# Issuing the load of the w2 sums for batch 14's last step behind the first eight adjacency rows of the final joined product

## The chip, the cores and the metric

The kernel runs on one core of a Trainium2 chip. The metric is the device time in microseconds of one execution; lower is better. The engines are named as in the profile: PE (matrix products; PEld is its weight load), DVE (vector), ACT (scalar, activations), POOL and SP. SP computes nothing here: it issues the DMAs, in the order in which the program names them.

## What is computed

For x of shape (16, 1024, 256), 16 batches of 1024 nodes with 256 channels, two layers run, each with a residual and a layer norm over the channels. The first is an attention whose queries come from a product with an adjacency matrix weighted by the likeness of the nodes. The second, in which the change lies, is a pair of graph convolutions:

```python
h = relu(x @ w1_loop + adj @ (x @ w1_neigh) + b1)      # 256 -> 128 channels
h = relu(h @ w2_loop + adj @ (h @ w2_neigh) + b2)      # 128 -> 256 channels
x = layernorm(x + (x + h) * 0.5)                       # adj is 1024 x 1024, the same for all batches
```

All is in float32.

## The kernel before

The batches pass through a pipeline written out by hand. While the attention of batch b runs, the first graph convolution of batch b-1 and the second of batch b-2 are computed together. Their common factor is the adjacency matrix, so the class `Joined` puts both into one block product by Strassen's scheme (in Winograd's form): the 2 x 2 blocks of the adjacency and four sums of these blocks are multiplied in seven products instead of eight. The eight factors of the adjacency lie in DRAM as `far_adj`, named "00", "01", "10", "11" (the blocks, transposed) and 1, 2, 3, 4 (their sums). Each is two tiles ("rows") of 128 x 1024 floats, 512 KB each. `fetch` (line 193) loads both tiles of a factor, one DMA each, issued by SP (line 198).

The last product of the second convolution, with w2, is done by the same scheme (`seventh_part`, line 967, and `last_products`, line 978). It needs four sums of blocks of w2 and one row of the bias, 320 KB in all, which were computed once at the start and lie in DRAM as `w2_sums`. `load_sums` (line 948) takes a row tile and loads them (line 950).

`Joined.run` (line 1137) goes in this order. Products 1, 2, 6, 7, 5, 4 and 3 (line 1134) read the factors "00", "10", 2, 3, 1, 4 and "11". Between them, functions of other stages are called from a table that the caller passes (`turn_to`). After product 2 the bias of the first half of the channels is put into the PSUM bank `third`, and `load_sums` is called for the older batch (`c2`). After product 4, `block_sums` (line 953) makes the left sums, and `bias(second, c2.b2_step)`, an ACT copy of line 1142, reads the fifth block of the loaded sums. Then come half of product 3, three steps of `last_products` (line 971 on PE, copies on ACT at lines 984, 989 and 992, additions on DVE at lines 986, 993 and 975), the other half of product 3, and the rest.

The final step, lines 1447 to 1461, has no attention beside it: `c1` is batch 15, `c2` batch 14, and `c3` and `c4` are batches 13 and 12, whose results still have to be normalized and stored. SP's order in this step is: fourteen adjacency tiles (line 1449), two more of block "01" (line 1450), the residual x of batch 14 (`c2.load_x`, line 850), the store of batch 12's result (`c4.finish`, line 1018), the residual x of batch 15 (`c1.load_x`, line 850), the sums of w2 (line 950), the store of batch 13's result (line 1018). The x tiles come from a pool of three buffers, so that batch 15's x takes the one from which batch 12's result is stored.

Row tiles, which hold adjacency tiles, sums, snapshots of PSUM and the like, come from a pool of 31 buffers of one size (`row_tile`, line 99), handed out in turn: the first instruction that writes a tile waits until the buffer's former content is no longer read. After the seven products, `ending` (line 1029) computes the second convolution of batch 15 and its layer norm, and stores it piece by piece.

Of the kernel before, what the change touches and what calls it, by code (L numbers as in the profile page):

```python
# [18 lines left out]
def kernel(  # L19
# [68 lines left out]
    def half_psum(name):  # L88
        return big_psum(name)[:, 0:FB]
# [4 lines left out]
    def load_x(b, name):  # L94
        xb = xpool.tile([P, NT, C], F32, tag="x", name=f"x_{name}")
        nc.sync.dma_start(out=xb, in_=x[b].rearrange("(t p) c -> p t c", p=P))
        return xb

    def row_tile(name):
        return work.tile([P, N], F32, tag="row", name=name, bufs=ROWS)  # L100
# [107 lines left out]
    def fetch_quarters(name, ready=None):  # L208
        return {ij: (ready or {}).get(n) or fetch(n, name) for ij, n in QUARTERS.items()}
# [67 lines left out]
    class NodeSums:  # L277


        def __init__(self, q, xb, name):  # L280
            self.q, self.name = q, name
            self.square = squares[len(taken) % 2]
            taken.append(name)
            q.c_col = self.square[:, 0:NT]
            for t in range(NT):
                nc.scalar.activation(xb[:, t, :], xb[:, t, :], AF.Identity, accum_out=self.square[:, t:t + 1])
# [118 lines left out]
    class KeysValues:  # L405
# [45 lines left out]
        def run(self, between=lambda: None, later=lambda: None):  # L451
            self.start()
            self.middle(between, later)
            return self.end()
# [387 lines left out]
    class GraphConv:  # L842


        def __init__(self, b, xT, nodes=None, x=None):
            self.b, self.xT, self.nodes, self.x = b, xT, nodes, x

        def load_x(self):
            self.x = xpool.tile([P, NT, C], F32, tag="x", name=f"x1_{self.b}")
# [253 lines left out]
    class Joined:  # L1103
# [33 lines left out]
        def run(self, between=None, last=None):  # L1137
            c1, c2, b = self.c1, self.c2, self.b
            between = between or {}

            def bias(bank, row):
                nc.scalar.copy(bank.rearrange("p (t c) -> p t c", c=P), row.unsqueeze(1).to_broadcast([P, TJ, P]))

            def turn_to(n):
                for f in between.get(n, ()):
                    f()

            first, third, second = (half_psum(f"hu_ps_{b}_{i}") for i in range(3))
            s12, s34 = (row_tile(f"snap_{b}_{k}") for k in range(2))
            p1, u1, u3, p7 = s12[:, 0:FB], s12[:, FB:N], s34[:, 0:FB], s34[:, FB:N]  # L1150
            c1.loop(third, 0, start=True)
            self.product(1, first, start=True)
            nc.scalar.copy(p1, first)
            turn_to(1)
            self.product(2, third)
            nc.vector.tensor_add(p1, p1, third)
            turn_to(2)
            if last:
                bias(third, b2_sb[:, ts(0, P)])
                c2.load_sums()  # L1160
            self.product(6, first, again=True)
            nc.scalar.copy(u1, first)
            c1.relu(0, p1)
            turn_to(6)
            self.product(7, second, start=True)
            nc.scalar.copy(p7, second)
            turn_to(7)
            self.product(5, first, again=True)
            nc.scalar.copy(u3, first)
            turn_to(5)  # L1170
            self.product(4, second, again=True)
            c2.uT = row_tile(f"uT_{c2.b}")
            add_upper = lambda: nc.vector.tensor_add(c2.uT[:, 0:FB], u1, second)
            add_lower = lambda: (last or nc.gpsimd).tensor_add(c2.uT[:, FB:N], u3, p7)
            if not last:
                add_upper()
                add_lower()
                turn_to(4)
                c1.loop(first, 1, again=True)
                self.product(3, first, again=True)  # L1180
                c1.relu(1, first)
                turn_to(3)
                return
            c2.block_sums(last, add_upper, add_lower)
            bias(second, c2.b2_step)
            turn_to(4)
            c1.loop(first, 1, again=True)
            self.product(3, first, again=True, steps=range(0, TJ // 2))
            rest = c2.last_products(third, second)
            self.product(3, first, again=True, steps=range(TJ // 2, TJ))  # L1190
            c1.relu(1, first)
            rest()
            turn_to(3)
            return third, second

    def run():
# [58 lines left out]
        for b in range(B):  # L1255
            more = b + 1 < B
            att = Attention(b, xB, qT, kT, v)
            c1, c2, c3 = (convs.get(b - k) for k in (1, 2, 3))
            both = Joined(c1, c2) if c2 else None
# [186 lines left out]
            convs[b] = GraphConv(b, norm.x1T, norm.nodes)  # L1446
        c1, c2, c3, c4 = (convs[B - k] for k in (1, 2, 3, 4))
        both = Joined(c1, c2)
        both.fetch("00", "10", 2, 3, 1, 4, "11")
        quarters = fetch_quarters("e", both.far)  # L1450
        c2.load_x()
        c1.inner()
# [10 lines left out]
    with tc.manual_schedule():  # L1463
        run()
# [67 lines left out]
```

## Time and profile before

| what | value |
|---|---|
| median of the runs | 2136.1 us |
| lowest and highest of 3 runs | 2135.74 and 2136.44 us |
| time of the profiled execution | 2135.35 us |
| span of the profiled execution | 2133.6 us |
| mean granted PE clock in it | 0.997 |
| PE busy | 2116.3 us (99%) |
| DVE busy | 1907.5 us (89%) |
| ACT busy | 1140.1 us (53%) |
| POOL busy | 359.0 us (17%) |
| DMA queue of the loads and stores | 61.2% of 16 engines |

The span runs from the first to the last instruction that the profile has; what lies around it is 1.75 us here. An engine's busy share is a mean over the whole program. All moments below are us from the start of the span. The final step, in which the change lies, covers roughly the last 78 us: its first adjacency load is issued at 2054.66 us.

### The profile page before, as it was taken

Reading aid. Unit: us, or ns where it says so; the run is one execution under the profiler, and the core shown is the slowest. Engines: PE = TensorE matmul, PEld = TensorE weight load, DVE = VectorE, ACT = ScalarE, POOL = GpSimd, SP = SyncE. Lnnn points to the kernel's source line nnn. Section 1 sums busy time; section 2 is a strip of 40 time slices with the busy share of each in tenths; the row PEclk is TensorE's granted clock in tenths of the full one; section 3 lists DMA queues with packets and bytes.
Section 4 is the critical chain, followed back from the end, with each engine's and each line's share of the span. In section 5 each row is a group of like instructions: output and inputs, shape, how many; then the busy total and the mean of one; then the engine's idle time right before and its main releaser. Section 6 shows DMA issues by size and latency. Waiting matters only on the chain.

```text
span 2133.6 us, 25172 instructions
## 1 busy us (share of the span) xinstructions
PE 2116.3 (99%) x8734; PEld 1037.2 (49%) x8734; DVE 1907.5 (89%) x2381; ACT 1140.1 (53%) x1669; POOL 359.0 (17%) x209
## 2 busy tenths in 40 slices
PE   9999999999999999999999999999999999999997
PEld 5344444545545455444454444544454444545454
DVE  7899999989999898998989989899898999989874
ACT  5745545556365563655635555454655546556322
POOL 2010120221303113031130301313012130221111
PEclk9999999999999999999999999999999999999998
DMA  9495666637549284592946829377293763925453
GB/s 222 120 170 193 135 221 146 186 107 141 203 125 272 74 165 169 137 262 70 201 141 150 241 69 233 109 163 228 75 259 103 153 212 106 268 87 107 165 192 112
DMA packets 613718, 346.39 MB, mean 162 GB/s; under 512 B 491984, under 2 KB 556880, under 8 KB 613584
## 3 DMA queue, kind: packets, MB, share of 16 engines
q1 hardware_dynamic: 613312, 344.45, 61.2%
q8 instruction: 71, 1.16, 0.2%
q14 instruction: 63, 0.52, 0.1%
q10 hardware_dynamic: 272, 0.26, 0.0%
HBM read 294.45 MB, written 50.20 MB: 162 GB/s over the span
## 4 chain that ended last, share of the span: by engine, by line
PE 98%; DMA 1%; DVE 1%; ACT 0%; POOL 0%; issue 0%; POOLq 0%; SPq 0%; ACTq 0%; DVEq 0%
PE s L702 21%; PE av L744 21%; PE g_ps L647 16%; PE hu_ps L1134 16%; PE v_ps L448 5%; PE k_ps L444 5%; PE hu_ps L971 4%; PE t_ps L857 3%; PE g_ps L574 3%; PE hu_ps L864 2%; PE h_ps L879 1%; PE u_ps L908 1%; DMA out_dram<-x 1%; PE h_ps L971 1%; DMA w_sums<-w_sums 0%; PE den_ps L764 0%
## 5 line engine op out<-in xcount | busy, mean ns | idle before, releaser
L723 DVE TENSOR_TENSOR acc<-acc,pr 128x1024 f32<-128x1024 f32 x384 | 472.2, 1230 | 37.4 <-DVE acc L723 1.4
L702 PE MATMUL s<-qT,kT 64*128 64x512 f32 x2048 | 449.7, 593 | 0.0
L744 PE MATMUL av<-pr,v 128*64 128x512 f32 x2048 | 447.0, 594 | 0.0
L709 ACT ACTIVATE pr<-s 128x1024 f32<-128x1024 f32 x392 | 390.7, 1115 | 75.6 <-PE s L702 75.6
L702 PEld LDWEIGHTS s<-qT,kT 64*128 64x128 f32 x2048 | 196.3, 187 | 232.7 <-issue 183.3
L744 PEld LDWEIGHTS av<-pr,v 128*64 128x64 f32 x2048 | 144.0, 137 | 297.4 <-issue 272.6
L361 POOL TENSOR_TENSOR rstd<-rstd,neg_half 128x32 f32<-128x32 f32 x16 | 99.3, 6203 | 1113.2 <-DVE rstd L359 1113.2
L1134 PE MATMUL hu_ps<-adj,R 128*128 128x512 f32 x480 | 214.3, 594 | 0.0
L560 ACT ACTIVATE wg<-c_row,c_sums 128x1024 f32<-128x1024 f32 x120 | 137.0, 1142 | 81.4 <-DVE den_part L731 60.3
L566 DVE SCALAR_TENSOR_TENSOR wg<-wg,adj 128x1024 f32<-128x1024 f32 x128 | 150.0, 1211 | 3.6 <-ACT wg L561 3.6
L707 ACT ACTIVATE pr<-s 128x512 f32<-128x512 f32 x240 | 142.4, 702 | 0.3 <-PE s L702 0.3
L1134 PEld LDWEIGHTS hu_ps<-adj,R 128*128 128x128 f32 x480 | 89.0, 190 | 100.9 <-issue 99.5
L561 ACT ACTIVATE wg<-wg 128x1024 f32<-128x1024 f32 x128 | 135.3, 1057 | 4.1
L860 ACT COPY t<-t_ps 128x1024 f32<-128x1024 f32 x16 | 16.2, 1012 | 189.6 <-PE t_ps L857 189.6
L647 PE MATMUL g_ps<-wg,S 128*128 128x512 f32 x224 | 115.5, 597 | 0.0
L647 PE MATMUL g_ps<-T,S 128*128 128x512 f32 x224 | 115.5, 597 | 0.0
L647 PE MATMUL g_ps<-wg,x 128*128 128x512 f32 x224 | 109.0, 599 | 0.0
L1134 PE MATMUL hu_ps<-adj,t 128*128 128x512 f32 x240 | 105.7, 592 | 0.0
L1125 POOL TENSOR_TENSOR R<-h 128x512 f32<-128x512 f32 x14 | 28.2, 2012 | 359.5 <-PE av L744 238.8
L721 DVE TENSOR_TENSOR acc<-pr,pr 128x1024 f32<-128x1024 f32 x64 | 77.5, 1211 | 12.3 <-ACT pr L709 12.3
L728 DVE STREAM_TRANSPOSE accB<-acc 128x1024 f32<-128x1024 f32 x64 | 79.7, 1245 | 2.2
L731 DVE TENSOR_REDUCE den_part<-accB 128x32 f32<-128x1024 f32 x64 | 78.1, 1220 | 2.2
(235 smaller groups left out, 3120.1 us busy)
## 6 DMA issues: line engine op xcount, KB each, us to landing
adj<-adjT SPq DMA_DIRECT2D x210, 512.0 KB
adj<-in_adj_dram SPq DMA_DIRECT2D x128, 512.0 KB
para<-in_L_gnn_para_dram SPq DMA_DIRECT2D x32, 512.0 KB
xB_a<-in_x_dram SPq DMA_DIRECT2D x128, 128.0 KB
x1d<-xB_a SPq DMA_DIRECT2D x128, 128.0 KB
x<-x1d SPq DMA_DIRECT2D x16, 1024.0 KB
xB<-in_x_dram SPq DMA_DIRECT2D x120, 128.0 KB
x<-in_x_dram SPq DMA_DIRECT2D x15, 1024.0 KB
```

Of the source, the lines that this page charges most:

```text
L444: nc.tensor.matmul(dst, self.a[0][n], self.w[n], start=not again, stop=True, skip_group_check=again)
L448: nc.tensor.matmul(dst[:, ts(t, P)], self.w[n][:, ts(t, P)], self.a[1][n], start=not again and t == 0, stop=True, skip_group_check=again o ...
L560: nc.scalar.activation(wg, self.c_row, AF.Abs, bias=self.c_col[:, t:t + 1], scale=-1.0)
L561: nc.scalar.activation(wg, wg, AF.Tanh, scale=-0.5 / C)
L566: nc.vector.scalar_tensor_tensor(wg, wg, 1.0, self.adj.pop(t), op0=ALU.add, op1=ALU.mult)
L647: nc.tensor.matmul(self.p[n], x_n[:, k, :], w_n, start=(k == 0), stop=(k == TJ - 1))
L702: nc.tensor.matmul(halves[s], self.kT[rows, pair, ts(mt, P)], self.qT[rows, pair, ts(j, FB)], start=True, stop=True)
L707: nc.scalar.activation(pr[:, ts(s, FB)], halves[s], AF.Exp)
L709: nc.scalar.activation(pr, ps, AF.Exp)
L723: nc.vector.tensor_add(self.acc, self.acc, prs[mt])
L744: nc.tensor.matmul(pav[s * HD:(s + 1) * HD, :], self.v[:, mt, pair * P + s * HD:pair * P + (s + 1) * HD], prs[mt][:, ts(s, FB)], start=(mt ...
L1134: nc.tensor.matmul(dst, self.x[n][:, k, :], of_rows(rows, k), start=(start and k == 0), stop=(k == TJ - 1), skip_group_check=again)
```

## The change

In the final step, `load_sums` for batch 14 is called when eight of the fourteen adjacency tiles ("00", "10", 2 and 3) have been issued, ahead of the six of 1, 4 and "11". `Joined.run` calls it only where it has not been called for this batch. In the steps before the final one nothing changes: there the sums are still loaded in `run`.

```diff
@@ class GraphConv
         def __init__(self, b, xT, nodes=None, x=None):
             self.b, self.xT, self.nodes, self.x = b, xT, nodes, x
+            self.w2 = None
 
         def load_x(self):
@@ class Joined, run
             turn_to(2)
             if last:
                 bias(third, b2_sb[:, ts(0, P)])
-                c2.load_sums()
+                if c2.w2 is None:
+                    c2.load_sums()
             self.product(6, first, again=True)
@@ the final step
         c1, c2, c3, c4 = (convs[B - k] for k in (1, 2, 3, 4))
         both = Joined(c1, c2)
-        both.fetch("00", "10", 2, 3, 1, 4, "11")
+        both.fetch("00", "10", 2, 3)
+        c2.load_sums()
+        both.fetch(1, 4, "11")
         quarters = fetch_quarters("e", both.far)
         c2.load_x()
```

The row tile of the sums is now the ninth that the final step takes, where it was the twenty-second; the tiles in between come one place later in the turn of the pool's buffers.

## The prediction

> **What bounds the kernel now.** I read the page first: PE is busy for 2116.3 us of a span of 2133.6 us, and the chain of work that ended last is PE for 98% of the span. So the change can only gain where PE stands still, and only the last step is touched. I therefore read the PE timeline from 2040 us to the end, for the last step and for the step before it, which runs the same code for batch 13.
>
> The PE timeline (start, us, engine, line, operation, count, and in brackets idle time and what ended it), first the earlier step, then the last one:
>
> ```profile
> 2047.44 1.05 PE L971 MATMUL hu_ps<-w2n_sb,uT 128*128 128x128 f32 x8
> 2048.33 1.06 PE L971 MATMUL h_ps<-w2l_sb,h1T 128*128 128x128 f32 x8
> 2049.23 2.98 PE L971 MATMUL hu_ps<-w_sums,last 128*128 128x128 f32 x24
> 2052.04 1.88 PE L1134 MATMUL hu_ps<-adj,R 128*128 128x512 f32 x4
> ...
> 2086.36 1.05 PE L971 MATMUL hu_ps<-w2n_sb,uT 128*128 128x128 f32 x8
> 2087.25 1.06 PE L971 MATMUL h_ps<-w2l_sb,h1T 128*128 128x128 f32 x8
> 2095.13 4.62 PE L971 MATMUL hu_ps<-w_sums,last 128*128 128x128 f32 x24 [6.83 <-ACT h L984]
> 2099.59 1.88 PE L1134 MATMUL hu_ps<-adj,R 128*128 128x512 f32 x4
> ```
>
> The same four groups stand in both; only in the last step is there a hole, 6.83 us ahead of the 24 products, and these then take 4.62 instead of 2.98 us. From 2040 to 2124 us PE has no other idle time of this size. The hole is put down to the ACT copy of line 984, so I read ACT's timeline:
>
> ```profile
> 2079.25 0.59 ACT L1169 COPY snap<-hu_ps 128x512 f32<-128x512 f32 x1 [2.85 <-PE hu_ps L1134]
> 2093.49 0.59 ACT L1142 COPY hu_ps<-w_sums 128x512 f32<-128x512 f32 x1 [13.65 <-DMA w_sums<-w_sums]
> 2094.01 0.58 ACT L904 COPY h<-h1n_ps 128x512 f32<-128x512 f32 x1
> 2094.49 0.59 ACT L984 COPY h<-hu_ps 128x512 f32<-128x512 f32 x1
> ```
>
> Line 984 was not late by itself: it stood in ACT's queue behind line 1142, the preload of a PSUM bank with the bias step, which waited 13.65 us for the sums of w2. Why these came so late is in the chain of waits in order of time (start, us, what):
>
> ```profile
> 2072.27 13.35 DMA out_dram<-x
> 2085.62 0.02 issue
> 2085.64 0.36 SPq L850
> 2086.00 0.05 issue
> 2086.05 0.02 SPq L950
> 2086.06 0.03 issue
> 2086.09 7.32 DMA w_sums<-w_sums
> ```
>
> SP's queue is in order. Line 850 loads the residual x of batch 15 into a buffer that batch 12's output store still reads until 2085.62; the load of the sums (line 950) needs nothing of that store, yet is issued behind it, and then takes 7.32 us beside a 1 MB load and a 1 MB store.
>
> **What the Trainium skill says.** "TensorE: Matmul & The Clock Gate", Part 1 (the HAM clock gate): after about 3.4 us idle the array falls to half clock, and needs about 3.4 us of work to come back. The windows of 1 us agree (busy us of PE, PEld, DVE, ACT, POOL, then the granted clock, DMA share, GB/s): idle from 2088.3, half clock from about 2091.8 (a mean of 0.92 in that window), full again at about 2098.7 (a mean of 0.66), 3.6 us after work resumed.
>
> ```profile
> 2090.00:2091.00 1.00, 0.00 (x0) 0.00 (x0) 0.00 (x0) 0.00 (x0) 0.00 (x0) 1.00 0.89 252
> 2092.00:2093.00 1.00, 0.00 (x0) 0.00 (x0) 0.00 (x0) 0.00 (x0) 0.00 (x0) 0.50 1.07 386
> 2097.00:2098.00 1.00, 1.00 (x6) 1.00 (x6) 0.00 (x0) 0.59 (x1) 0.00 (x0) 0.50 0.00 0
> 2099.00:2100.00 1.00, 1.00 (x8) 0.78 (x8) 0.00 (x0) 0.21 (x1) 0.00 (x0) 1.00 0.00 0
> ```
>
> "DMA: Bandwidth & Descriptors", Anatomy of one DMA: a semaphore wait happens on the issuing sequencer before dispatch, so a waiting issue holds all behind it. The 13.35 us above agree. The same page, Issuing engines are not separate DMA queues: all DMAs share 16 engines. Agreed too: the adjacency loads alone run at 401 to 422 GB/s from 2061 to 2077 us with the DMA share at 1.0.
>
> **The change part by part.**
>
> 1. *The late load goes.* Line 950 is skipped in this step's run, so line 1142 needs only what it needs in the earlier step: PSUM bank `second` free, that is, DVE's line 1173 (2083.61, 0.69 us). It runs at about 2084.35 to 2084.95, line 904 to 2085.5, and ACT is free. In the earlier step line 984 starts 1.14 us after the first group of 8 products starts (2048.58 against 2047.44) and the 24 products start 1.79 us after it. So here: copy at 2087.50, products at 2088.15 instead of 2095.13, which is 6.98 us. No hole above 3 us is left, so the clock stays full, and the 24 products reach line 1134 in 2.81 us (2052.04 - 2049.23) instead of 4.46 (2099.59 - 2095.13), which is 1.65 us. From there to the transposes of line 903 it takes 3.50 us in the last step and 3.51 in the earlier one. Sum 8.63 us. As a check over the whole piece: 2103.09 - 2086.36 = 16.73 against 2055.55 - 2047.44 = 8.11, a difference of 8.62.
>
> 2. *The early load comes.* One more issue on SP, 0.32 us (median of 15; 0.53 in the last step), and 320 KB. SP's timeline shows that fourteen loads issue from 2054.66 and that from the ninth on each waits for an earlier one to land. For instance, in answers of narrow windows:
>
> ```profile
> 2060.48 0.32 SPq L198 DMA_DIRECT2D adj<-adjT  x1
> ...
> 2061.79 0.32 SPq L198 DMA_DIRECT2D adj<-adjT  x1
> ```
>
> These waits (8 of together 6.6 us, the longest 0.9) cover the issue. In the semaphore times of the trace each load's landing releases the issue eight places later, so first half row "00" landed at 2060.4, and the others follow every 1.28 us: the ninth ("1", first half) at about 2070.6, the eleventh ("4") at 2073.2, the thirteenth ("11") at 2075.8. The sums take the ninth place; at 410 GB/s 320 KB are 0.8 us. They land at about 2070.2, 14 us before 2084.35. What stands behind them moves by 0.8 us: row "1" is read from 2075.6 (2079.05 less product 5's 3.44), so 5.0 us of slack; "4" from 2079.05, 5.9; "11" from 2084.64, 8.9. None is used up: cost nothing. Without that cover each late us would be one us on PE.
>
> 3. *SP behind the loads.* The load of batch 14's x (issued 2070.65) and batch 12's store (2072.27, which also waits for DVE's normalization, ended 2072.24) move by up to 0.8 us. The former must land before DVE's line 975, now 2095.83, then about 2088.9; all traffic then queued has landed by 2085.62, so by 2086.4. The load of batch 15's x goes out at about 2086.4 without the sums beside it and lands near 2093; its reader is line 1054, now 2115.81, then 2107.2. The store behind it has no reader. POOL issues no transfer, and no instruction of it is moved.
>
> 4. *Buffers.* The sums take a row tile eight places into the list, so each of the six other adjacency tiles, the two "01" tiles, t1, R and the snapshots takes the buffer that its follower had. I count the 31 in turn: the latest release among these is the earlier step's R, third and fourth sums, read by product 3 until about 2053.9, and the old sums of w2, read until 2054.8 and now under the second snapshot, first written after 2075. SP reaches the first load at 2054.66 and the shifted ones after 2060. Cost nothing; were one held later, SP would pass that wait on.
>
> 5. *The tail.* From 2103 us PE sets the chain up to 2122.7, then statistics and the last stores, each released by the piece before. Nothing there is tied to a fixed moment except batch 15's x, above. So it moves as a whole.
>
> Profiled execution: span 2133.6 - 8.6 = 2125.0; its time 2135.35 - 8.6 = 2126.7. The median of the runs shown is 2136.1, 0.75 above the profiled one: 2127.5.
>
> Unknown costs. The half-clock term depends on where the idle stretch lies in the gate's window: at least about 1.0 and at most 2.3 us (half of 4.62), so 1.65 by -0.65 and +0.65. The new load in the stream: 0.8 us each row, or at worst the 7.32 it took in traffic; I take 0.8, as the stream is in order and full. A gain from it I exclude: it only adds bytes.
>
> **The rivals.**
> - *Partly given back* (0.08): the sums' rows of 2.5 KB move as slowly as in the last step, 7.3 us, and rows behind come 7.3 late. Slack 5.0, so PE stands 2.3 us at product 5: gain 6.3, about 2129.8. For it: no view shows this load in a full stream of adjacency rows. Against it: the 7.32 us were shared with 2 MB of other traffic.
> - *The wait changes its name* (0.04): batch 14's x lands after DVE needs it, or ACT waits for something else until about 2093, and the gain is under 0.2%, say 2135. Against it: x has 2.5 us to spare, and PE's products don't read it.
> - *Slower* (0.02): SP is held at the moved load, or the load drags, and product 5's row comes late. It costs nothing up to 5.0 us of delay, then one for one, and passes the gain from 5.0 + 8.6 = 13.6 us; at 16 us the time is 2138.5. Nothing in the trace holds a buffer so long: what is read after 2057 belongs to later places in the turn.
>
> **How the numbers follow.** The forecast case, all of the stall gone, has 0.86, its own range 2126.5 to 2128.6 from the clock term and the scatter of the runs. Stretched into the partial case it becomes 2126.3 to 2129.4, with less than 2 in 10 outside. A difference of about 0.2% (4.3 us) is what a measurement of this kernel can tell. The forecast and the partial case are faster by more: 0.94; same 0.04; slower 0.02.
>
> **What would show it.** In the changed profile the 24 products should start within 0.3 us after the group before them and take about 3.0 us, the clock stay at 1.00 there, line 1142 wait on DVE, not on a DMA, and no gap open at line 1134 between 2068 and 2082. Wrong if PE idles at product 5 or 4 on a load, if the clock still falls to 0.50, or if line 1054 waits on batch 15's x.

## The result and the profile after

| what | before | changed |
|---|---|---|
| median (6 runs each) | 2135.93 us | 2126.92 us |
| lowest and highest | 2135.5 and 2136.91 us | 2126.55 and 2127.59 us |
| span of the profiled execution | 2133.6 us | 2125.2 us |
| mean granted PE clock in it | 0.997 | 0.999 |

The ratio is 0.9957, with a 95% interval of [0.9944, 0.997]: the change makes the kernel 9.0 us faster, where 8.6 were forecast.

PE's timeline of the changed kernel, the same four groups as before, and the transposes behind them (line numbers are one higher than before from line 847 on, and two higher from line 1161 on):

```profile
2087.04 1.05 PE L972 MATMUL hu_ps<-w2n_sb,uT 128*128 128x128 f32 x8
2087.93 1.06 PE L972 MATMUL h_ps<-w2l_sb,h1T 128*128 128x128 f32 x8
2088.82 2.98 PE L972 MATMUL hu_ps<-w_sums,last 128*128 128x128 f32 x24
2091.64 1.88 PE L1135 MATMUL hu_ps<-adj,R 128*128 128x512 f32 x4
...
2095.14 0.60 PE L904 MATMUL h1n_ps<-ident,h1T 128*128 128x128 f32 x4
```

No bracket stands behind the 24 products any more: they start 1.78 us after the first group (1.79 forecast) and take 2.98 us. From the first group to the transposes it is 2095.14 - 2087.04 = 8.10 us. In the kernel before the transposes stood here:

```profile
2103.09 0.60 PE L903 MATMUL h1n_ps<-ident,h1T 128*128 128x128 f32 x4
```

There it was 2103.09 - 2086.36 = 16.73 us. The difference is 8.63 us, the sum of the prediction.

ACT's timeline of the changed kernel shows what the bias copy waits for now:

```profile
2079.93 0.58 ACT L1171 COPY snap<-hu_ps 128x512 f32<-128x512 f32 x1 [2.85 <-PE hu_ps L1135]
2084.95 0.59 ACT L1143 COPY hu_ps<-w_sums 128x512 f32<-128x512 f32 x1 [4.43 <-DVE uT L1175]
2085.47 0.58 ACT L905 COPY h<-h1n_ps 128x512 f32<-128x512 f32 x1
2088.17 0.58 ACT L985 COPY h<-hu_ps 128x512 f32<-128x512 f32 x1 [2.12 <-issue]
```

It is DVE's addition that frees the bank, not the load, and ACT then stands ready 2.12 us before PE has something to copy. The chain of waits of the changed kernel runs through this piece on PE alone (start, us, what); the store, the two issues and the load that stood in it are gone:

```profile
2087.20 0.89 PE hu_ps L972 x8
2088.09 0.89 PE h_ps L972 x8
2088.98 2.82 PE hu_ps L972 x24
2091.80 1.72 PE hu_ps L1135 x4
```

SP itself still waits for batch 12's store, for 10.0 us where it was 9.9, but nothing that PE needs soon stands behind this wait any more. And the windows of the changed kernel show the clock at 1.00 (sixth value) over the place where it was at 0.50:

```profile
2088.00:2090.00 2.00, 2.00 (x19) 1.98 (x19) 0.89 (x2) 0.58 (x1) 0.00 (x0) 1.00 0.68 153
2090.00:2092.00 2.00, 2.00 (x17) 1.83 (x16) 0.49 (x1) 0.75 (x2) 0.00 (x0) 1.00 0.99 286
2092.00:2094.00 2.00, 2.00 (x10) 1.21 (x9) 1.38 (x2) 0.87 (x2) 0.00 (x0) 1.00 1.06 374
```

Where the sums landed can be read from SP, since each landing releases the issue eight places later. Two lines of SP's timeline of the changed kernel, the second tile of block "01" and batch 14's x, and then PE's line of products 6, 7 and 5:

```profile
2070.67 0.32 SPq L198 DMA_DIRECT2D adj_e<-adjT  x1
...
2071.95 0.37 SPq L851 DMA_DIRECT2D x<-x1d  x1
```

```profile
2069.43 10.46 PE L1135 MATMUL hu_ps<-adj,R 128*128 128x512 f32 x24
```

The first was released by the sums, which so landed at 2070.66, 14.3 us before ACT reads them. The second was released by the first half of row "1", at 2071.94. Its reader is product 5, the last 8 of these 24 records. The 16 of products 6 and 7 ahead of it take 6.87 us, as the 16 of products 1 and 2 do (2069.43 - 2062.56), so product 5 starts at 2069.43 + 6.87 = 2076.30, and the row has 4.4 us to spare. This number is used below.

The two profiled spans differ by 8.4 us, not 8.63. Everything ahead of this piece came 0.68 us later in the changed kernel's profiled execution (the first group at 2087.04 for 2086.36), and the last store took some 0.5 us less. Such scatter is seen without the change too: in the kernel before and in three experiments that differ from it only later, the first group starts between 2086.36 and 2087.38. The medians' difference is 0.4 us larger than 8.63, which is well within its interval.

### The profile page after: what moved, and what is told of

It is laid out like the page before. It is cut to its first block, busy times and chain, and to the rows that moved or that the text cites. A ratio compares the mean times of both kernels' runs of the same rounds, so it can differ in the third digit from the quotient of the medians.

```text
span 2125.2 us, 25170 instructions
## 1 busy us (share of the span) xinstructions
PE 2115.0 (100%) x8734; PEld 1036.0 (49%) x8734; DVE 1907.4 (90%) x2381; ACT 1139.7 (54%) x1669; POOL 358.6 (17%) x209
## 4 chain that ended last, share of the span: by engine, by line
PE 97%; SPq 1%; DMA 1%; DVE 0%; ACT 0%; issue 0%; POOL 0%; POOLq 0%; DVEq 0%
PE s L702 21%; PE av L744 21%; PE hu_ps L1135 17%; PE g_ps L647 16%; PE v_ps L448 4%; PE k_ps L444 4%; PE hu_ps L972 4%; PE t_ps L858 3%; PE hu_ps L865 2%; PE g_ps L574 1%; PE h_ps L880 1%; PE u_ps L909 1%; PE h_ps L972 1%; SPq L108 1%; SPq L229 0%; DMA adj<-in_adj_dram 0%
## 5 line engine op out<-in xcount | busy, mean ns | idle before, releaser
L721 DVE TENSOR_TENSOR acc<-pr,pr 128x1024 f32<-128x1024 f32 x64 | 77.5, 1210 | 11.9 <-ACT pr L709 11.9
```

## The experiments

The theory: the sums were late because SP, which issues in order, could not issue the load of batch 15's x before batch 12's store had landed (this wait is called the hold below), and the sums stood behind it. That cost the hole in PE, and the hole cost the clock. Nine kernels were run, each against the kernel before on the same chip.

### Late in the queue, but ahead of the hold

```diff
-        both.fetch("00", "10", 2, 3)
-        c2.load_sums()
-        both.fetch(1, 4, "11")
+        both.fetch("00", "10", 2, 3, 1, 4, "11")
...
         c4.finish(out[B - 4])
+        c2.load_sums()
         c1.load_x()
```

> Against the changed kernel, one thing differs: in the final step the sums are issued behind all sixteen adjacency tiles, batch 14's x and batch 12's store, but ahead of the load of batch 15's x, which waits for that store. Theory (the cost was the place behind the load of batch 15's x, which SP can't issue until the store has landed): SP issues the sums at about 2076, they land with the traffic queued ahead of them by about 2086.5, ACT's preload ends about 2087.1, and PE idles at most 0.5 us before the 24 products; clock at 1.00; gain 8 to 8.6 us against before, about 2127.5 us. Rival (any place late in the queue is too late, the early landing is what counts): the sums still land some 7 us after their need, the hole stays above 3 us, the clock falls, and the gain is under 4 us, about 2132 us or more.

Measured: 2126.92 us against 2135.98, ratio 0.9957 [0.994, 0.9973]. ACT's timeline of this kernel, and PE's first group:

```profile
2086.36 0.59 ACT L1143 COPY hu_ps<-w_sums 128x512 f32<-128x512 f32 x1 [6.35 <-DMA w_sums<-w_sums]
2086.88 0.58 ACT L905 COPY h<-h1n_ps 128x512 f32<-128x512 f32 x1
2087.66 0.59 ACT L985 COPY h<-hu_ps 128x512 f32<-128x512 f32 x1 [0.20 <-ACT h L905]
```

```profile
2086.52 1.05 PE L972 MATMUL hu_ps<-w2n_sb,uT 128*128 128x128 f32 x8
```

Here ACT does wait for the load, for 6.35 us, and it costs nothing: line 985 starts 1.14 us after PE's first group, as it does without any wait, and ACT stood idle for 0.20 us before it. So the place behind eight rows is one of many. The sums landed at 2086.28 by the semaphore times, and about 0.2 us later would still have done; one place further back in SP's queue, in the kernel before, they land at 2093.41, 7 us later.

### The same place in the program, another queue

```diff
-                c2.load_sums()
+                c2.load_sums(nc.sync if last is nc.vector or b < B - 1 else nc.scalar)
```

(`load_sums` takes the issuing engine as an argument here.)

> The kernel before with one edit: in the final step the sums are issued by ACT, at the place in the program where they always were. Theory (SP's order is the cause, not the place in the program): ACT issues them at about 2073.5, behind its first bias copy, and they land long before 2084.3 beside batch 14's x and batch 12's store; no hole at the 24 products, gain 8 to 8.6 us, about 2127.5 us, less up to 0.5 us if the issue itself delays ACT's snapshots of products 6 and 7. Rival (the transfer in traffic is what costs): they land more than 10 us after issue, later than 2084.3, and most of the hole stays; 2131 us or more.

Measured: 2126.96 us, ratio 0.9957 [0.9941, 0.9974]. ACT's timeline, around the issue and at the bias copy:

```profile
2073.35 0.35 ACTq L950 DMA_DIRECT2D w_sums<-w_sums  x1
2073.74 0.58 ACT L1162 COPY snap<-hu_ps 128x512 f32<-128x512 f32 x1 [0.21 <-issue]
...
2084.38 0.59 ACT L1142 COPY hu_ps<-w_sums 128x512 f32<-128x512 f32 x1 [4.48 <-DVE uT L1173]
```

By the semaphore times the load lands at 2081.13, 7.8 us after its issue, which is no shorter than the 7.32 us before. The time of the transfer stays and the cost is gone: SP's order was the cause, not the transfer. The issue costs ACT 0.2 us ahead of a copy that has time. No row tile changes its place in the turn of the buffers in this kernel, so the same gain comes without any change of the buffers.

### PE kept busy through the hole

```diff
             self.seventh_part(2, d, start=True)
...
+            if aside is not None:
+                for _ in range(56):
+                    nc.tensor.transpose(aside, ident, ident)
             self.seventh_part(6, a)
```

> The kernel before, with 56 transposes of the identity added on PE in front of the 24 products in the final step only; they write an unused half of a PSUM tile and take about 6.2 us of the 6.83 us hole. The late load stays as it is. Theory (1.65 us of the stall is the clock that falls to half while PE idles): the clock stays at 1.00 through the hole, the 24 products reach line 1134's successor in about 2.8 us instead of 4.46, and the time is 1.65 us below before, about 2134.3 us. Rival (the 24 products are slow for another reason, such as waits between them and ACT's copies): they still take about 4.5 us and the time stays at 2135.9 us, or rises by what the added products overrun the hole.

Measured: 2133.96 us against 2135.98, ratio 0.999 [0.9981, 0.9999]. PE's timeline of this kernel:

```profile
2088.41 6.28 PE L990 MATMUL hu_ps<-ident 128*128 128x128 f32 x56
2095.47 2.99 PE L971 MATMUL hu_ps<-w_sums,last 128*128 128x128 f32 x24 [0.77 <-ACT h L984]
2098.29 1.88 PE L1137 MATMUL hu_ps<-adj,R 128*128 128x512 f32 x4
```

The load is as late as before, as its chain of waits shows:

```profile
2086.37 7.37 DMA w_sums<-w_sums
```

But the 24 products take 2.99 us instead of 4.62 and reach the next group in 2.82 us instead of 4.46, and the windows from 2084 to 2104 all show a clock of 1.00. That is the 1.64 us of the clock, shown by itself. The median fell by 2.0 us; its interval, 0.2 to 4.1 us, holds the 1.64. Work without any use made the kernel faster. It agrees with "TensorE: Matmul & The Clock Gate", Part 1, in the Trainium skill, by which the clock is set by how busy PE has been lately.

### Why the load takes 7.3 us

```diff
-        7: (lambda: c3.finish(out[B - 3]),)
+        7: (lambda: normalize(c3.mv, c3.rstd, c3.x),), 3: (lambda: c3.store(out[B - 3]),)
```

> The kernel before, except that the store of batch 13's result, which SP issues 0.6 us behind the sums, is issued after the last products instead; everything ahead of the sums stays. Rival of the theory on the 7.32 us of the load (it is that long because of what is issued behind it): the sums land about 3.3 us of data plus some 2 us after the load of batch 15's x was issued at 2085.6, by about 2091 instead of 2093.4, the hole shrinks by some 2.4 us to about 4.5 us, and the time is about 2133.5 us. Theory as the prediction has it (traffic already queued and the load of batch 15's x make the 7.32 us; what comes behind doesn't hold a load up): the load still takes about 7 us and the time stays at 2135.9 us within 0.7.

Measured: 2136.18 us, ratio 1.0003 [0.9994, 1.0012]. This doesn't test the rival, since the edit didn't do what it was meant to do. The store was called later in the program, but SP computes nothing and waits only for the normalization, so it issued the store 0.62 us behind the sums, as before:

```profile
2086.62 0.53 SPq L950 DMA_DIRECT2D w_sums<-w_sums  x1
2087.24 0.39 SPq L1021 DMA_DIRECT2D out_dram<-x  x1
```

In the second form the store goes through ACT's queue, which has copies ahead of it:

```diff
-3: (lambda: c3.store(out[B - 3]),)
+3: (lambda: c3.store(out[B - 3], nc.scalar),)
```

> The kernel before, except that batch 13's result is stored by ACT's queue, behind its last copies, so that SP has nothing behind the load of the sums; the order ahead of the sums stays. Theory as the prediction has it (a load is not held up by what is issued behind it): the sums still land 7 us after their issue and the time stays at 2135.9 us within 0.7. Rival (the 7.3 us are due to the 1 MB store issued 0.6 us behind): 1.3 MB at 410 GB/s are 3.3 us[...], so they land about 5.3 us after the issue of batch 15's x, 2 us earlier; the hole shrinks to under 5 us, and the time is near 2133.7 us.

Measured: 2134.62 us against 2135.87, ratio 0.9994 [0.9985, 1.0003]. The load in the chains of waits, first form and second:

```profile
2086.62 7.16 DMA w_sums<-w_sums
```

```profile
2086.66 5.98 DMA w_sums<-w_sums
```

Both explanations were half right. In these profiles a store issued 0.6 us behind the load made it 1.2 to 1.4 us longer (7.16, 7.32 and 7.37 us with it, 5.98 without); the other 6.0 us remain with nothing behind it. Most of them go to batch 15's x, issued 0.45 us ahead: in the windows of 2 us from 2086 on this profile shows 56, 284, 342 and 6 GB/s, together 1.38 MB, of which x is 1.05 and the sums 0.33. No kernel was run without that load ahead. The sums land 6.4 us after x's issue, where the rival expected 5.3 and the kernel before has 7.8. (The 2 us that the expectations add to the data are rather much: in the changed kernel's tail a 256 KB store with nothing else in flight, issued at 2114.45, lands at 2116.60, its data included.) PE's hole is 5.03 us in this profile, and the gain of 1.25 us in the medians is of the size of the shorter load, but its interval reaches 1, so a gain in time is not shown.

### First of all

```diff
-        both.fetch("00", "10", 2, 3)
-        c2.load_sums()
-        both.fetch(1, 4, "11")
+        c2.load_sums()
+        both.fetch("00", "10", 2, 3, 1, 4, "11")
```

> The changed kernel with the sums issued as the very first load of the final step, ahead of all adjacency tiles. Theory (each tile has slack, so 0.8 us more costs nothing anywhere): row '00' lands about 0.8 us later, at 2061.3 to 2061.7, its first reader on PE starts near 2062.2, and the time is that of the changed kernel, 2126.9 us within 0.5. Rival (the first rows have no slack; the place behind eight rows matters): PE idles up to 1 us at product 1, 2127.5 to 2128 us.

Measured: 2126.76 us, ratio 0.9956 [0.9939, 0.9972]. PE's timeline at product 1:

```profile
2060.69 1.88 PE L865 MATMUL hu_ps<-x1T,w1l_sb 128*128 128x512 f32 x4
2062.41 7.03 PE L1135 MATMUL hu_ps<-adj,t 128*128 128x512 f32 x16
```

Product 1 follows the group before it without idle time. So the first rows have 0.8 us to spare too.

### A dear load in the same place

The sums are read from a second copy in DRAM, cut into pieces of 8 or of 4 floats. The lines that make the copy, in the step before, are left out here.

```diff
+            if cut:
+                nc.sync.dma_start(out=dst.rearrange("p (n r) -> p n r", r=8), in_=pieces)
```

> The changed kernel, but the sums are read from a copy in DRAM that is cut into pieces of 32 bytes, 10240 of them (the copy is made in the step before, while no other transfer runs). By the 128-byte pieces of batch stores ahead of this step, about 1.1 us for 1024 pieces, this is some 11 us of the 16 engines instead of 0.8. Theory (a delay of the rows behind costs nothing up to the slack, then one for one): in the changed kernel row '1' lands 4.4 us before product 5 starts, so PE stands about 11 - 0.8 - 4.4 = 5.8 us at product 5, and with the fallen clock up to 1.7 us more; 2132.5 to 2134.5 us, still under the kernel before. Rival (there is more cover than that, or the load is no dearer in small pieces): no idle at product 5, 2127 us.

Measured: 2128.38 us, ratio 0.9965 [0.9951, 0.9979], 1.5 us above the changed kernel. PE's timeline at product 5, and SP's issue that waits for the first half of row "1":

```profile
2068.75 7.03 PE L1141 MATMUL hu_ps<-adj,R 128*128 128x512 f32 x16
2076.46 3.67 PE L1141 MATMUL hu_ps<-adj,R 128*128 128x512 f32 x8 [0.68 <-ACT snap L1176]
```

```profile
2076.48 0.61 SPq L853 DMA_DIRECT2D x<-x1d  x1
```

By the semaphore times the pieces took 5.16 us behind the row ahead of them, not the 11 us expected, so the size was wrong by half, and the time lies below the 2132.5 us of the theory and above the 2127 of the rival. The row behind landed at 2076.32; SP was busy with another issue until 2076.44. Product 5 would have started at 2068.75 + 6.87 = 2075.62 and started at 2076.46, 0.84 us late; the row landed 0.70 us too late, and PE starts 0.14 us after a landing here as it does in the last experiment. (This profile is of the fastest of the five runs.) The bracket names an ACT copy that ends at nearly the same moment, but product 5 neither reads nor overwrites what that copy touches; of several things waited for, the bracket shows only the last. During the load the windows show 59 to 62 GB/s where whole rows show 407 to 412. That small pieces are slow is stated in "DMA: Bandwidth & Descriptors", Specifications, which asks for 512 B at least.

> The same with 20480 pieces of 16 bytes, some 22 us by the same rate. Theory: PE stands about 22 - 0.8 - 4.4 = 16.8 us at product 5, plus up to 1.7 us by the clock, and the kernel is slower than before: 2143.5 to 2145.5 us. Whatever the load takes, the time should lie above the changed kernel's by its delay less 4.4 us, and pass that of the kernel before where the delay passes about 13 us. Rival (part of the delay is taken up elsewhere): less than that by more than 2 us.

Measured: 2158.16 us, ratio 1.0103 [1.0086, 1.012]. The total can't be read as was intended. The second copy, made in the step before, was not done in time: its own 16-byte writes kept the DMA engines busy at 7 to 10 GB/s from 2026 to 2066, so that all rows came late and PE idled at product 1 as well. PE's timeline:

```profile
2083.20 9.92 PE L1141 MATMUL hu_ps<-adj,t 128*128 128x512 f32 x16 [20.85 <-DMA adj<-adjT]
2092.95 7.03 PE L1141 MATMUL hu_ps<-adj,R 128*128 128x512 f32 x16
2105.87 5.40 PE L1141 MATMUL hu_ps<-adj,R 128*128 128x512 f32 x8 [5.89 <-DMA adj<-adjT]
2111.11 3.60 PE L1141 MATMUL hu_ps<-adj,h 128*128 128x512 f32 x8
```

The second hole is the one that was wanted, and can be read by itself: product 5 comes 2105.87 - (2092.95 + 6.87) = 6.05 us late and then takes 5.24 us (to 2111.11) instead of 3.43. So a hole on this side of the balance costs the clock as well, 1.81 us. Behind the first hole the 16 records take 2092.95 - 2083.20 = 9.75 us instead of 6.87, which is 2.88 us.

### The hold put ahead of the rows

```diff
         both.fetch("00", "10", 2, 3)
         c2.load_sums()
-        both.fetch(1, 4, "11")
-        quarters = fetch_quarters("e", both.far)
+        block01 = fetch("01", "e")
...
         c1.load_x()
+        both.fetch(1, 4, "11")
+        quarters = fetch_quarters("e", {**both.far, "01": block01})
```

> The changed kernel with the six adjacency tiles of 1, 4 and '11' issued last, behind the load of batch 15's x, which waits for batch 12's store: the hold that the sums stood behind in the kernel before now stands ahead of these tiles. By the traces so far the store is issued at about 2073.3 and lands some 6 us later (less is queued ahead of it), batch 15's x goes out at about 2080, and row '1' lands behind it at about 2085 to 2086, where product 5 would start at 2076.3. Theory (a row that is late costs one for one from its slack of 4.4 us on, and a hole[...] costs up to 1.8 us more by the clock): PE idles 9 to 10 us at product 5, the product's 8 records take about 5.4 us instead of 3.6, and the time is the changed kernel's plus 10.5 to 12 us: 2137.5 to 2139 us, slower than before. Rival (one for one without the clock, so that the gain is only passed at 13.6 us of delay): no lengthened product, 2136 to 2137 us. Second rival (the shorter queue ahead of the store brings it home early and the rows with it): under 2133 us.

Measured: 2139.1 us against 2135.99, ratio 1.0015 [1.0008, 1.0022]: slower than before, and 0.1 us above the range that the theory gave. The chain of waits, then PE's timeline:

```profile
2072.51 6.12 DMA out_dram<-x
2078.65 0.36 SPq L851
...
2079.10 6.49 DMA adj<-adjT
2085.59 0.14 issue
```

```profile
2068.99 7.03 PE L1135 MATMUL hu_ps<-adj,R 128*128 128x512 f32 x16
2085.73 5.26 PE L1135 MATMUL hu_ps<-adj,R 128*128 128x512 f32 x8 [9.71 <-DMA adj<-adjT]
2090.82 3.60 PE L1135 MATMUL hu_ps<-adj,h 128*128 128x512 f32 x8
```

It is the chain of the kernel before with another load at its end: store, held issue, load, hole in PE. Product 5 comes 2085.73 - (2068.99 + 6.87) = 9.87 us late and takes 2090.82 - 2085.73 = 5.09 us instead of 3.43. That is 11.5 us in all; the profiled span is 11.2 us longer than the changed kernel's and the median 12.2 us. Batch 12's store takes 6.12 us here, where it took 13.35 in the kernel before. By the semaphore times it lands 2.6 us after batch 14's x in both; the rest of its time is the queue ahead of it, which is six tiles shorter here.

## Why the prediction was right, and where it was off

1. *The late load goes.* Right to a tenth of a microsecond: 8.63 us in the piece, where 8.63 was forecast. Both terms were shown apart. The hole goes when the load is taken out from behind the hold, by either of two other ways (ahead of it, or by ACT), and the clock term of 1.65 us is there when PE is kept busy through the hole (1.64 us). That fit is one of two profiles: the clock term in it is the one that the prediction read from this same profile of the kernel before. The six holes in the profiles of these runs cost between 1.35 and 2.88 us by the clock (last section), so that the medians agree nearly as well may be partly luck. Of the prediction's bounds for the term, the 1.0 us is given without working, and "half of 4.62" is no upper bound, since 24 products that take 2.81 us at full clock could take 2.81 us more at half.

2. *The early load comes.* Right: the sums' landing at 2070.66 was forecast at about 2070.2 in a step that began 0.68 us earlier. Row "1" kept 4.4 us, where 5.0 less the 0.8 of the load were expected. No PE idle opens between products 1 and 3.

3. *SP behind the loads.* Right: batch 15's x is issued at 2086.97 and its reader, line 1055, runs at 2107.87 and waits for PE. DVE's line 976 reads batch 14's x at 2089.80 without a wait.

4. *Buffers.* Right as far as the trace shows: SP's waits in this step are those for earlier loads, for DVE's normalization and for the store. No kernel was run that changes the buffers' turn and nothing else, but the load issued by ACT, which leaves the turn as it was, gains the same 9.0 us.

5. *The tail.* From the transposes on, every group of PE stands 7.95 us earlier, as the transposes do.

The 401 to 422 GB/s that the prediction reads as agreeing with shared engines show only that SP's loads by themselves fill the 16 engines. That a load of another engine shares them is seen when ACT issues the sums: from 2072 to 2078 the traffic stays at 406 to 414 GB/s, as in the kernel before, and the load takes 7.8 us.

The rivals. *Partly given back* has its mechanism shown with another size: a load that took 5.2 us in this place cost 0.84 us at product 5, so the price, one for one past the slack, is right but for the 0.14 us, and the sums in their usual rows don't reach it. *The wait changes its name* fell: ACT's wait on DVE ends before PE needs it. *Slower* has its place and mechanism shown in the last experiment, but its point was put wrong. The prediction said that a late row costs "one for one" and passes the gain from "5.0 + 8.6 = 13.6 us". The term missing from that sum is the clock, which the same prediction had counted in the hole it removed: the hole of the last experiment costs 1.66 us more on this side too. Counted as in the prediction, from where the row lands in the kernel before, the point is then 5.0 + 8.6 - 1.66 = 11.9 us instead of 13.6. Counted from where it lands in the changed kernel, with 4.4 us of slack left, it is 4.4 + 8.63 - 1.66 = 11.4 us. Both are estimates worked out from these runs, not run themselves, and no better than the clock term. In the last experiment the row was 9.73 + 4.4 = 14.1 us later than in the changed kernel, 2.7 us past the point, and the kernel is slower than before by 3.1 us.

## What to carry to other kernels

When an engine idles on a small load, look at what stands ahead of that load in the issuing queue and what this waits for; the transfer time may be innocent. The three places ahead of the held issue that were tried did equally well (2126.76 to 2126.92 us), since what they pushed back kept its slack. When a hole in PE is priced, count the stretch at half clock behind it, for the hole that goes and for any that may come, and as a range: here it was 1.35 to 2.88 us.

## What was not expected of the hardware

What a hole costs by the clock doesn't follow its length. Holes of 5.03, 5.89, 6.30, 6.83, 9.71 and 20.85 us made the products behind them 1.35, 1.81, 1.81, 1.65, 1.66 and 2.88 us longer. (5.89 and 20.85 are the 16-byte kernel's. 6.30 and 5.03 are those of the first and second form with the later store, where the 24 products reach the next group in 4.63 and 4.17 us instead of 2.82.) Two windows of the second form show the fall and the return of the clock, the third value from the end, and then two of the last experiment:

```profile
2092.00:2094.00 2.00, 0.00 (x0) 0.00 (x0) 0.00 (x0) 1.28 (x3) 0.00 (x0) 0.97 0.02 6
2096.00:2098.00 2.00, 2.00 (x15) 2.00 (x14) 0.00 (x0) 0.58 (x1) 0.00 (x0) 0.68 0.00 0
```

```profile
2078.00:2079.00 1.00, 0.00 (x0) 0.00 (x0) 0.00 (x0) 0.00 (x0) 1.00 (x1) 0.84 0.01 5
2088.00:2089.00 1.00, 1.00 (x2) 0.34 (x1) 0.00 (x0) 0.00 (x0) 0.00 (x0) 0.54 1.05 422
```

By these means the clock was at half from 2093.88 to 2097.28, 3.4 us, and from 2078.68 to 2088.92, 10.2 us; in the kernel before it was so from 2091.84 to 2098.68, 6.8 us. That is once, three times and twice the same 3.4 us. PE had been idle for 4.6, 2.7 and 3.5 us when the clock fell, and the clock came back 2.9, 3.2 and 3.6 us after work resumed.

- A load was made 1.2 to 1.4 us longer by a 1 MB store that was issued 0.6 us behind it on the same queue (7.16 to 7.37 us in three profiles with it, 5.98 in one without).
- A load issued by ACT at 2073.35 landed at 2081.13, and batch 12's store, issued by SP at 2072.34, landed at 2087.17: the later one on the other queue overtook it.
- Reading 320 KB in pieces of 32 bytes took 5.2 us in the stream. Writing it in pieces of 16 bytes kept the DMA engines busy for over 40 us.
